# Six row buffers before the scatter, router products in three places, and two groups of stores on other queues, in a gated attention and expert layer

## The chip, the cores and the metric

The kernel runs on one core of a Trainium2 chip. A core has five engines that work side by side and wait for each other through semaphores: TensorE (PE, matrix products), VectorE (DVE), ScalarE (ACT), GpSimd (POOL) and SyncE (SP). Copies between the memory outside (DRAM) and the core (SBUF) are DMAs; each is issued by an instruction on the queue of SP, ACT or POOL, and all of them move through the same 16 DMA engines. Each engine takes its instructions in order. The metric is the device time of one execution in microseconds (us), lower is better.

## The reference: what is computed

The input `x` has 4096 rows of 512. An attention block with a context of 3202 rows comes first, then a layer of eight experts of which each row uses two.

```
Sim  = hc@w1 + hq@w2 + (hc*w3)@hq.T + b          # hc = layernorm(x), hq = context
hq_hat = softmax(Sim) @ hq
hc_bar = softmax(max(Sim)) @ hc                  # one row
x1   = x + tanh(g) * (concat[hc, hq_hat, hc*hq_hat, hc*hc_bar] @ W_qv + b_qv)
logits = layernorm(x1) @ w_router + b_router     # 8 experts, the best 2 of each row
buf[expert, slot] = row                          # a fixed number of slots per expert
out  = x1 + tanh(g2) * (weighted sum of the two experts' gelu MLPs)
```

The capacity of an expert is 1.25 * 4096 / 8 = 640 rows here, in five tiles of 128; a row beyond it is dropped. All arithmetic is in float32.

## The kernel before

The work stands in three parts. Part one (lines 124 to 808) is the attention. The 4096 rows are taken in eight groups `g` of 512, and for each group there are these stages:

- `stage_s(g)` (line 425) computes the transposed similarities `E` for 13 blocks of the context, in seven pairs, by a seven-product scheme (`chain`, line 394), and the column maxima `M`. After the last pair, the maxima are transposed on TensorE (`mps`, line 472), reduced on VectorE (`mt`), spread again by a product with a diagonal (`mbps`, from `diag_rows`, line 155) and copied by ScalarE to `mb`.
- `stage_e(g)` (line 498) subtracts `mb` on VectorE and takes the exponential on ScalarE, tile by tile.
- `stage_v(g)` (line 556) multiplies by the context rows (`vv` for group 0, line 568). ScalarE copies the result to `hqT`, and VectorE forms `hqT*qT` and four sums `hs` (lines 654 to 662).
- `stage_d(g - 1)` (line 697) is the product with `W_qv`; its result `xs` goes to DRAM as `r_d`, four DMAs for a group (line 754).

Group 0 has extra work, because the derived operands that later groups read from DRAM are made there. During `stage_v(0)`, `build_values` and `left_sums` (lines 343 and 333) load 13 pairs of context row tiles (`vcv`), form four sums (`vsv`) on VectorE and store them as `vs_d`. `build_weights` (line 345) does the same four times with rows of `W_qv` (`wc`, `wt`, stored as `wt_d`). The buffers of `vcv` and `wc` are two, and so are those of `vsv` and `wt`. The 21 stores are issued from ScalarE's queue, in between its arithmetic.

`router_weights` (line 228) multiplies the four 512-row parts of `W_qv` by the router weights, so that the logits come out beside `x1` later. For each part there are 16 products of 128x128 by eight columns, all into one PSUM bank `we`. In the kernel before, part 0 stands right after the last similarity, part 1 after the four transposes, and parts 2 and 3 after the diagonal product, all ahead of `vv`. The operands are loaded into SBUF tiles that are not yet used for anything else (tags `hqT`, `xr`, `T2`, `hs`).

Part two (lines 826 to 1044) is the second half of `x1` and the routing. It runs over 32 row tiles in nine steps (seven of four tiles and two of two). For each tile, `tile_mm` (line 872) loads `r` and, once for four tiles, `q2T`; TensorE makes eight products (`x1p`, line 885), VectorE finishes `x1` and its statistics, and ScalarE's queue stores `x1` to `out`. For each step, `norms` (line 906) computes the scale on GpSimd (`rstd`) and writes the normalised rows to `xn`, `route` (line 922) finds the two experts on VectorE, and `dispatch` (line 1017) scatters the rows to their slots in `buf_d` by eight indirect DMAs on GpSimd's queue, two for each tile. The loop at line 1035 calls `norms` for step `g`, then `dispatch` for step `g - 2`, then `route` for step `g - 1`. `xn` has three buffers, the default of the pool. Beside its rows each `xn` holds the token's number, copied there by VectorE (line 1002). The weights of the first expert are loaded along the way, one half after `q2T` 3 and one after `q2T` 6.

Part three (lines 1052 to 1267) runs the eight experts; its loads of `buf_d` wait for all scatters.

What stands where in each engine's queue is decided by a scheduler when the program is built; `tc.issue_after` places an instruction no earlier than another.

Of the kernel before, what the change touches and what calls it, by code (L numbers as in the profile page):

```python
# [6 lines left out]
F32 = mybir.dt.float32  # L7
# [7 lines left out]
P = 128  # L15
# [5 lines left out]
def gated_layer(ctx, tc, x, x_t, ctxt, ctxt_t, g_xattn, g_ffn, w_sim, w_sim1, b_sim, W_qv, W_qv_t, b_qv, b_qv_c, w_router, b_router, w1, b1, w2, b2, out):  # L21
# [14 lines left out]
    TG = 4 * P  # L36

    BW = D // 2 + E // 2
    B1 = D // 2 + E
    NG = N // TG  # L40
# [29 lines left out]
    r_d = [dram.tile([P, 2, BW], F32, name=f"r_d{t}", tag=f"r_d{t}") for t in range(NT)]  # L70

    R = D + 4
# [19 lines left out]
    we = const.tile([P, 4, DC, E], F32, name="we")  # L92
# [31 lines left out]
    with ExitStack() as s1:  # L124
        ee = s1.enter_context(tc.tile_pool(name="ee", bufs=1))
        kv = s1.enter_context(tc.tile_pool(name="kv", bufs=1))
        st = s1.enter_context(tc.tile_pool(name="st", bufs=5))
        sb = s1.enter_context(tc.tile_pool(name="sb1", bufs=1))
# [12 lines left out]
        wt_d = dram.tile([P, 8, DC, BW], F32, name="wt_d", tag="wt_d")  # L141
# [6 lines left out]
        def bank(name):  # L148
            return ps_m.tile([P, 2, 256], F32, name=name, tag="m")
# [10 lines left out]
        live = {}  # L160
# [66 lines left out]

        def router_weights():

            pa_ = sb.tile([P, DC, TG], F32, name="wq0", tag="hqT")  # L230
            pb_ = sb.tile([P, 4, 2, BW], F32, name="wq1", tag="xr").rearrange("p a b c -> p (a b c)")[:, : DC * D]
            parts = [[(pa_, 0, D)], [(pb_.rearrange("p (c f) -> p c f", c=DC), 0, D)], [], []]
            for c in range(DC):
                t2 = ee.tile([P, 2, 256], F32, name=f"wq2_{c}", tag=f"T2{c}").rearrange("p a b -> p (a b)")
                parts[2].append((t2.rearrange("p (c f) -> p c f", c=DC), c * P, P))
            for i, k in enumerate((2, 4)):
                parts[3].append((sb.tile([P, DC, 256], F32, name=f"wq3_{i}", tag=f"hs{k}"), i * 256, 256))
            ps = bank("we").rearrange("p a b -> p (a b)")[:, : 4 * DC * E].rearrange("p (k c e) -> p k c e", k=4, c=DC)
            for k, pieces in enumerate(parts):
                for a, f0, n in pieces:  # L240
                    with tc.issue_after(queue[-1].ins):
                        nc.sync.dma_start(a, W_qv_t[:, :, k * D + f0 : k * D + f0 + n])

            def step(ks):
                for k in ks:
                    for a, f0, n in parts[k]:
                        for f in range(n // P):
                            for d in range(DC):
                                nc.tensor.matmul(
                                    ps[:, k, (f0 // P) + f, :], a[:, d, f * P : (f + 1) * P], wrc[:, d, :],  # L250
                                    start=k == 0 and f == 0 and d == 0, stop=d == DC - 1, skip_group_check=True,
                                )

            return step, lambda: nc.vector.tensor_copy(we, ps)

        def stage_n(g):

# [75 lines left out]
        def left_sums(name, w, vc, dst):  # L333

            vs = sb.tile([P, 4, 256], F32, name=f"vs{name}", tag="vs", bufs=2)
            A11, A21, A12, A22 = (vc[:w, h, c : c + 256] for h in range(2) for c in (0, 256))
            tt(vs[:w, 0, :], A21, A22, ALU.add)
            tt(vs[:w, 1, :], vs[:w, 0, :], A11, ALU.subtract)
            tt(vs[:w, 2, :], A11, A21, ALU.subtract)
            tt(vs[:w, 3, :], A12, vs[:w, 1, :], ALU.subtract)  # L340
            nc.scalar.dma_start(dst, vs[:w])

        def build_values(j):

# [2 lines left out]
        def build_weights(c):  # L347


            vc = sb.tile([P, 2, 2, BW], F32, name=f"wc{c}", tag="vc", bufs=2)  # L350
            for h in range(2):
                with tc.issue_after(queue[-1].ins):
                    nc.sync.dma_start(
                        vc[:, h, :, :256],
                        W_qv[(h + 1) * D + c * P : (h + 1) * D + (c + 1) * P, :].rearrange("p (j d) -> p j d", j=2),
                    )
            nc.vector.tensor_copy(vc[:, :, :, 256:], we[:, 1:3, c, :].rearrange("p h (j e) -> p h j e", j=2))
            nc.scalar.dma_start(wt_d[:, 0:4, c, :], vc.rearrange("p h j d -> p (h j) d"))
            B11, B12, B21, B22 = (vc[:, h, j, :] for h in range(2) for j in range(2))
            wt = sb.tile([P, 4, BW], F32, name=f"wt{c}", tag="vs", bufs=2)  # L360
            tt(wt[:, 0, :], B12, B11, ALU.subtract)
            tt(wt[:, 1, :], B22, wt[:, 0, :], ALU.subtract)
            tt(wt[:, 2, :], B22, B12, ALU.subtract)
            tt(wt[:, 3, :], B21, wt[:, 1, :], ALU.subtract)
            nc.scalar.dma_start(wt_d[:, 4:, c, :], wt)

        def load_keys(g, j):
            kt = st.tile([P, 7, 2, WJ[j]], F32, name=f"kt{g}_{j}", tag="st")
# [56 lines left out]
        def stage_s(g):  # L425
# [39 lines left out]
                    for h in (1, 0):  # L465
                        tt(m, m, e[:w, :, h], ALU.max)  # L466
            if g == 0:
                rw, rw_end = router_weights()
                rw([0])
            ps = ps_tr.tile([P, 4, P], F32, name=f"mps{g}", tag="tr")  # L470
            for i in range(4):
                tr = nc.tensor.transpose(ps[:, i, :], M[:, i // 2, 0, (i % 2) * P : (i % 2 + 1) * P], ident)
            if g == 0:
                with tc.issue_after(tr.ins):
                    rw([1])
            mt = sm.tile([P, 4], F32, name=f"mt{g}", tag="mt")
            nc.vector.tensor_reduce(mt, ps, AX.X, ALU.max)
            ps = ps_tr.tile([P, 4, P], F32, name=f"mbps{g}", tag="tr").rearrange("p a b -> p (a b)")
            dr = diag_rows(ps, f"m{g}", mt)
            if g == 0:  # L480
                with tc.issue_after(dr.ins):
                    rw([2, 3])

            m = sm.tile([P, 4], F32, name=f"m{g}", tag="mm")
            stt(m, qw[:, 4 * g : 4 * g + 4], bsim, mt, ALU.add, ALU.add)
# [7 lines left out]
            nc.scalar.copy(mb.rearrange("p a b -> p (a b)"), ps)  # L493
            live[g]["mt"], live[g]["mb"] = mt, mb
            if g == 0:
                live[g]["we"] = rw_end

        def stage_e(g, first):

# [56 lines left out]
        def stage_v(g, early, between):  # L556
# [6 lines left out]
            def product(ps, what, right, start=True, stop=True):  # L563
                for i in range(2):
                    vt = load_values(g, what, i)
                    for j in range(i * JH, min((i + 1) * JH, NJ)):
                        for b in range(2):
                            nc.tensor.matmul(  # L568
                                ps[b], vt[: WJ[j], j - i * JH, b * P : (b + 1) * P], right(j),
                                start=start and j == 0 and (b == 0 or g == 0), stop=stop and j == NJ - 1,  # L570
                                skip_group_check=True,
                            )

            if g == 0:
                with tc.issue_after(v["last"].ins):
                    v["we"]()
                for i in range(2):
                    ps = [bank(f"vv{i}_{b}") for b in range(2)]
                    for h in range(2):
                        product(  # L580
                            ps, (h, i * 256), lambda j: E[j // 2][: WJ[j], :, h, j % 2, :], start=h == 0, stop=h == 1
                        )
# [114 lines left out]
        def stage_d(g):  # L697
# [53 lines left out]
            prod(pb, "3", start=False)  # L751
            out_sum(pb, u2, 0, 1)
            for i in range(4):
                nc.sync.dma_start(r_d[4 * g + i], xs[:, i, :, :])

# [69 lines left out]
    G = 4  # L825
    with ExitStack() as s2:
# [79 lines left out]
        def norms(k, x1s, mv, lg):  # L906
            n = len(x1s)
            rstd = sm.tile([P, G], F32, name=f"rstd{k}", tag="rstd")[:, :n]
            nc.gpsimd.tensor_scalar(rstd, mv[:, :n, 1], EPS, None, ALU.add)
# [413 lines left out]
```

## Time and profile before

| | |
|---|---|
| median of 3 runs | 2747.27 us (2743.96 to 2749.41) |
| the profiled execution | 2750.92 us |
| its span, first to last instruction | 2749.1 us |
| TensorE busy | 2656.2 us (97%) |
| VectorE busy | 1689.9 us (61%) |
| ScalarE busy | 420.0 us (15%) |
| GpSimd busy | 219.8 us (8%) |
| mean rate of DMA over the span | 159 GB/s |

The profile page and the answers of its trace are about one execution. Times are in microseconds from the start of the span. A row of the timeline has the start, the duration, the engine, the line of the kernel, the operation, what it writes and what it reads, how many such instructions in a row, and in brackets the idle time before it with what ended it. SPq, ACTq and POOL rows with DMA are DMAs as they are issued. A float32 product counts as two matmul rows. PEclk is the share of TensorE's full clock that was granted. A row of the list of waits names the engine and line that waited, what it waited for, the sum, how many times, and the longest.

### The profile page before, as it was taken

How to read it: one execution, taken by the hardware profiler on the slowest of the kernel's cores; microseconds unless marked ns; L12 is line 12 of the kernel's file. 1: busy time of each engine (PE TensorE's matmuls, PEld its weight loads, DVE VectorE, ACT ScalarE, POOL GpSimd, SP SyncE). 2: the span in 40 equal slices, each digit the busy share in tenths (PEclk: the TensorE clock that was granted, in tenths of full speed). 3: DMA queues.
4: the chain of work that ended last, by engine and by line, in shares of the span. 5: the costliest groups of instructions: out<-in, count | busy, mean ns of one | idle time of the engine just before them, and what ended most of it. 6: DMA issues, size and time to landing. Idle time of an engine off the chain costs nothing. (4 is left out here: it accounts for less than half of the span.)

```text
span 2749.1 us, 29996 instructions
## 1 busy us (share of the span) xinstructions
PE 2656.2 (97%) x11384; PEld 2139.7 (78%) x11384; DVE 1689.9 (61%) x3410; ACT 420.0 (15%) x673; POOL 219.8 (8%) x268
## 2 busy tenths in 40 slices
PE   8999999999999999999999985699999999999998
PEld 7847888888888888888888774477777777777776
DVE  6755755946847559468374556555656475756654
ACT  1200200201202002012020011111111212111111
POOL 0000000000001000000000035201010010101010
PEclk9799999999999999999999998899999999999999
DMA  6876766646747657467445684223233231423210
GB/s 250 247 265 216 173 221 156 227 157 175 233 163 173 219 152 231 158 174 231 150 144 180 243 310 156 91 77 100 92 103 118 86 123 62 146 85 108 78 61 20
DMA packets 191908, 436.64 MB, mean 159 GB/s; under 512 B 18599, under 2 KB 95648, under 8 KB 189716
## 3 DMA queue, kind: packets, MB, share of 16 engines
q1 hardware_dynamic: 158114, 358.54, 41.3%
q0 software_dynamic: 13648, 36.55, 4.2%
q10 hardware_dynamic: 20001, 39.63, 3.9%
q8 instruction: 90, 1.47, 0.2%
q14 instruction: 55, 0.44, 0.0%
HBM read 356.22 MB, written 85.60 MB: 161 GB/s over the span
## 5 line engine op out<-in xcount | busy, mean ns | idle before, releaser
L448 PE MATMUL pas<-Qp,kt 128*128 128x256 f32 (+1 forms) x728 | 174.1, 380 | 0.0
L1085 PE MATMUL pah<-bT,w 128*128 128x320 f32 x512 | 160.1, 435 | 0.8 <-DVE bT L1126 0.8
L568 PE MATMUL pbv<-E,vt 128*128 128x256 f32 (+1 forms) x728 | 159.5, 379 | 0.0
L568 PEld LDWEIGHTS pbv<-E,vt 128*128 128x128 f32 (+1 forms) x728 | 138.2, 190 | 18.9
L448 PEld LDWEIGHTS pas<-Qp,kt 128*128 128x128 f32 (+1 forms) x728 | 135.2, 187 | 21.3 <-ACT p1s L405 0.2
L885 PE MATMUL x1p<-W,q2T 128*128 128x264 f32 x512 | 126.6, 411 | 18.9 <-DVE mv L903 12.4
L508 DVE TENSOR_TENSOR E<-E,mb 128x1024 f32<-128x1024 f32 (+1 forms) x112 | 125.0, 1140 | 17.3 <-ACT mb L493 17.3
L509 ACT ACTIVATE E<-E 128x1024 f32<-128x1024 f32 (+1 forms) x112 | 111.4, 996 | 156.4 <-DVE E L508 154.0
L885 PEld LDWEIGHTS x1p<-W,q2T 128*128 128x128 f32 x512 | 103.3, 204 | 39.9 <-issue 20.8
L1085 PEld LDWEIGHTS pah<-bT,w 128*128 128x128 f32 x512 | 97.5, 191 | 39.9 <-DVE bT L1126 1.2
L1085 PE MATMUL pao<-w,h 128*128 128x256 f32 x512 | 121.0, 379 | 0.0
L1237 PE MATMUL op<-w,h 128*128 128x512 f32 x256 | 113.6, 592 | 0.0
L466 DVE TENSOR_TENSOR M<-M,E 128x1024 f32<-128x1024 f32 (+1 forms) x96 | 109.0, 1135 | 6.4
L1260 POOL DMA_INDIRECT out<-acc,ti x40 | 42.8, 1070 | 855.9 <-DVE acc L1259 855.9
L1085 PEld LDWEIGHTS pao<-w,h 128*128 128x128 f32 x512 | 96.7, 190 | 16.7 <-issue 4.3
L405 ACT COPY p1s<-pas 128x512 f32<-128x512 f32 (+1 forms) x56 | 31.1, 555 | 488.4 <-issue 256.7
L421 DVE TENSOR_TENSOR E<-p4s,u3s 128x512 f32<-128x512 f32 (+1 forms) x56 | 36.5, 652 | 107.4 <-PE p4s L448 107.4
L448 PE MATMUL pbs<-Qp,kt 128*128 128x256 f32 (+1 forms) x364 | 88.0, 384 | 4.0 <-DVE E L416 4.0
L520 DVE TENSOR_TENSOR SM<-SM,E 128x1024 f32<-128x1024 f32 (+1 forms) x80 | 88.8, 1110 | 0.0
L1237 PEld LDWEIGHTS op<-w,h 128*128 128x128 f32 x256 | 47.2, 190 | 52.0 <-issue 46.4
L448 PE MATMUL p6s<-q,kt 128*128 128x256 f32 (+1 forms) x364 | 86.6, 379 | 0.0
L448 PE MATMUL pbs<-q,kt 128*128 128x256 f32 (+1 forms) x364 | 86.6, 379 | 0.0
(406 smaller groups left out, 5240.5 us busy)
## 6 DMA issues: line engine op xcount, KB each, us to landing
kt<-kt_d SPq DMA_DIRECT2D x84, 896.0 KB
w<-in_w SPq DMA_DIRECT2D x32, 2048.0 KB
wp<-wt_d SPq DMA_DIRECT2D x56, 520.0 KB
vt<-vs_d SPq DMA_DIRECT2D x28, 896.0 KB
vt<-vs_d SPq DMA_DIRECT2D x28, 640.0 KB
kt_d<-ktb ACTq DMA_DIRECT2D x12, 896.0 KB
buf_d<-zero SPq DMA_DIRECT2D x80, 129.0 KB
xb<-buf_d SPq DMA_DIRECT2D x40, 258.0 KB
```

The lines of the kernel that those rows point to most:

```text
L405: nc.scalar.copy(p1, cut(pa))
L421: tt(done(1, 0), cut(p4), u3, ALU.add)
L448: nc.tensor.matmul(ps[:w, jl, :], kts[j][:, KSLOT[p], k, :], B[p][:, k, :], start=start and jl == 0 and k == 0, stop=stop and k == 1, skip ...
L466: tt(m, m, e[:w, :, h], ALU.max)
L508: live[g]["last"] = tt(e, e, m, ALU.subtract)
L509: live[g]["exp"] = nc.scalar.activation(e, e, AF.Exp)
L520: tt(s, E_t[0][:, lr] if jj == 1 else s, e, ALU.add)
L568: nc.tensor.matmul(ps[b], vt[: WJ[j], j - i * JH, b * P : (b + 1) * P], right(j), start=start and j == 0 and (b == 0 or g == 0), stop=stop ...
L885: nc.tensor.matmul(ps[:, j, :B1], qTs[g][:, c, i * P : (i + 1) * P], W1[:, c, j, :], start=(c == 0), stop=(c == DC - 1))
L1085: nc.tensor.matmul(ps, a, b, start=start and i == 0, stop=stop and i == len(A) - 1, skip_group_check=True)
L1237: nc.tensor.matmul(ps, hT[:, k, 2 * MH :], W2[:, k, :], start=(k == 0), stop=(k == KH - 1))
L1260: sc = nc.gpsimd.indirect_dma_start(out=out[:, :], out_offset=rows_of(ti, s), in_=acc[:, :], in_offset=None, bounds_check=N - 1, oob_is_er ...
```

## The change

There are four edits.

- `xn` gets six buffers.
- The router products are made in three places. Part 1 stands right after the last similarity, part 2 after the diagonal product, both into a bank `we12`; parts 0 and 3 follow the last `vv` product of group 0, into a bank `we03`, ahead of the row sums `rsps` and of `stage_s(1)`. The loads go in the order 1, 2, 0, 3, into other tags than before. In place of one copy of the bank to `we` there are three copies on VectorE, two of them at the end of `stage_v(0)`.
- The 13 stores of `vs_d` and the eight of `wt_d` are issued from GpSimd's queue.
- The four stores of `r_d` of the last group are issued from ScalarE's queue.

```diff
@@ router_weights @@
-            pa_ = sb.tile([P, DC, TG], F32, name="wq0", tag="hqT")
...
+            parts = [[], [], [], []]
+            a = sb.tile([P, DC, TG], F32, name="wq1", tag="hqT")
+            parts[1].append((a, 0, D))
+            a = sb.tile([P, 4, 2, BW], F32, name="wq2", tag="xr").rearrange("p a b c -> p (a b c)")[:, : DC * D]
+            parts[2].append((a.rearrange("p (c f) -> p c f", c=DC), 0, D))
+            for i, k in enumerate((2, 4)):
+                parts[0].append((sb.tile([P, DC, 256], F32, name=f"wq0_{i}", tag=f"hs{k}"), i * 256, 256))
             for c in range(DC):
...
+                parts[3].append((t2.rearrange("p (c f) -> p c f", c=DC), c * P, P))
+            for k in (1, 2, 0, 3):
...
-            def step(ks):
+            def step(ps, ks, first=True):
...
+        def we_bank(name):
+            return bank(name).rearrange("p a b -> p (a b)")[:, : 4 * DC * E].rearrange("p (k c e) -> p k c e", k=4, c=DC)
@@ left_sums @@
-            nc.scalar.dma_start(dst, vs[:w])
+            nc.gpsimd.dma_start(dst, vs[:w])
@@ build_weights @@
-            nc.scalar.dma_start(wt_d[:, 0:4, c, :], vc.rearrange("p h j d -> p (h j) d"))
+            nc.gpsimd.dma_start(wt_d[:, 0:4, c, :], vc.rearrange("p h j d -> p (h j) d"))
...
-            nc.scalar.dma_start(wt_d[:, 4:, c, :], wt)
+            nc.gpsimd.dma_start(wt_d[:, 4:, c, :], wt)
@@ stage_s @@
-                rw, rw_end = router_weights()
-                rw([0])
+                rw, rps = router_weights(), we_bank("we12")
+                rw(rps, [1])
...
-            if g == 0:
-                with tc.issue_after(tr.ins):
-                    rw([1])
...
                 with tc.issue_after(dr.ins):
-                    rw([2, 3])
+                    rw(rps, [2], False)
@@ stage_v @@
                 with tc.issue_after(v["last"].ins):
-                    v["we"]()
+                    nc.vector.tensor_copy(we[:, 1:3], rps[:, 1:3])
...
+                with tc.issue_after(vv.ins):
+                    rps = we_bank("we03")
+                    rw(rps, [0])
+                    rw(rps, [3], False)
+                    nc.vector.tensor_copy(we[:, 0], rps[:, 0])
+                    nc.vector.tensor_copy(we[:, 3], rps[:, 3])
                 between()
@@ stage_d @@
-                nc.sync.dma_start(r_d[4 * g + i], xs[:, i, :, :])
+                (nc.scalar if g == NG - 1 else nc.sync).dma_start(r_d[4 * g + i], xs[:, i, :, :])
@@ norms @@
-            xg[k] = sb.tile([P, G, R], F32, name=f"xn{k}", tag="xn")
+            xg[k] = sb.tile([P, G, R], F32, name=f"xn{k}", tag="xn", bufs=6)
```

More of the change, by code (lines that the diff above doesn't have):

```diff
@@ L228, in router_weights @@
         def router_weights():
-            pa_ = sb.tile([P, DC, TG], F32, name="wq0", tag="hqT")
-            pb_ = sb.tile([P, 4, 2, BW], F32, name="wq1", tag="xr").rearrange("p a b c -> p (a b c)")[:, : DC * D]
-            parts = [[(pa_, 0, D)], [(pb_.rearrange("p (c f) -> p c f", c=DC), 0, D)], [], []]
-            for c in range(DC):
[L234 to L240, printed above, removed]
+            parts = [[], [], [], []]
[5 more added lines that the diff above has]
+                parts[0].append((sb.tile([P, DC, 256], F32, name=f"wq0_{i}", tag=f"hs{k}"), i * 256, 256))
+            for c in range(DC):
+                t2 = ee.tile([P, 2, 256], F32, name=f"wq3_{c}", tag=f"T2{c}").rearrange("p a b -> p (a b)")
+                parts[3].append((t2.rearrange("p (c f) -> p c f", c=DC), c * P, P))
+            for k in (1, 2, 0, 3):
+                for a, f0, n in parts[k]:
                     with tc.issue_after(queue[-1].ins):
                         nc.sync.dma_start(a, W_qv_t[:, :, k * D + f0 : k * D + f0 + n])
-            def step(ks):
+            def step(ps, ks, first=True):
                 for k in ks:
@@ L250, in step @@
                                     ps[:, k, (f0 // P) + f, :], a[:, d, f * P : (f + 1) * P], wrc[:, d, :],
-                                    start=k == 0 and f == 0 and d == 0, stop=d == DC - 1, skip_group_check=True,
-                                )
-            return step, lambda: nc.vector.tensor_copy(we, ps)
+                                    start=first and k == ks[0] and f0 == 0 and f == 0 and d == 0, stop=d == DC - 1,
+                                    skip_group_check=True,
+                                )
+            return step
+        def we_bank(name):
+            return bank(name).rearrange("p a b -> p (a b)")[:, : 4 * DC * E].rearrange("p (k c e) -> p k c e", k=4, c=DC)
         def stage_n(g):
@@ L495, in stage_s @@
             if g == 0:
-                live[g]["we"] = rw_end
+                live[g]["we"] = rw, rps
         def stage_e(g, first):
@@ L567, in product @@
                         for b in range(2):
-                            nc.tensor.matmul(
+                            mm = nc.tensor.matmul(
                                 ps[b], vt[: WJ[j], j - i * JH, b * P : (b + 1) * P], right(j),
@@ L572, in product @@
                             )
+                return mm
             if g == 0:
+                rw, rps = v["we"]
                 with tc.issue_after(v["last"].ins):
-                    v["we"]()
+                    nc.vector.tensor_copy(we[:, 1:3], rps[:, 1:3])
                 for i in range(2):
@@ L579, in stage_v @@
                     for h in range(2):
-                        product(
+                        vv = product(
                             ps, (h, i * 256), lambda j: E[j // 2][: WJ[j], :, h, j % 2, :], start=h == 0, stop=h == 1
```

## The prediction, as put on record

> **What bounds the kernel now.** I read the page's 40 slices first. TensorE is full except in three places: the slice from about 1580 to 1760 us, its neighbours, and a dip of its clock near 100 to 140 us.
>
> ```profile
> PE   8999999999999999999999985699999999999998
> PEclk9799999999999999999999998899999999999999
> DMA  6876766646747657467445684223233231423210
> ```
>
> So the page says "TensorE-bound", and only these places have time to give. In each I look for the wait that ends last. For 1540 to 1740, the list of waits of that stretch has two entries that hold TensorE back and that this change touches:
>
> ```profile
> DVE xn L1002 <- DMA buf_d<-xn,sidx: 35.1, 5, 11.0
> PE x1p L885 <- DMA q2T<-qT_d: 5.3, 1, 5.3
> ```
>
> The first is VectorE, held at the copy of the token number until the scatter three steps back has landed. The timeline shows one step on GpSimd and VectorE:
>
> ```profile
> 1592.76 0.22 POOL L909 TENSOR_SCALAR rstd<-mv 128x4 f32<-128x4 f32 x1 [12.89 <-DVE tmp L984]
> 1598.53 1.15 POOL L1020 DMA_INDIRECT buf_d<-xn,sidx  x1 [4.44 <-DVE mv L903]
> 1607.69 0.97 POOL L1020 DMA_INDIRECT buf_d<-xn,sidx  x1 [0.30 <-issue]
> 1614.76 0.17 DVE L1002 COPY xn<-tok 128x4 f32<-128x4 f32 x1 [10.46 <-DMA buf_d<-xn,sidx]
> 1616.66 0.23 POOL L909 TENSOR_SCALAR rstd<-mv 128x4 f32<-128x4 f32 x1 [8.00 <-DVE tmp L984]
> ```
>
> GpSimd ends its eight scatters at 1608.66, idles 8.00 us, and starts the next `rstd` after VectorE is freed. The second wait starts on SP, whose queue has `r_d` stores ahead of the first `q2T` load:
>
> ```profile
> 1535.56 3.83 SPq L754 DMA_DIRECT2D r_d<-xr  x3
> 1539.48 0.38 SPq L876 DMA_DIRECT2D q2T<-qT_d  x1
> ```
>
> Around 100 us, TensorE's own timeline:
>
> ```profile
> 101.29 4.62 PE L249 MATMUL we<-wrc,wq 128*128 128x8 f32 x32
> 105.76 1.09 PE L472 MATMUL mps<-ident,M 128*128 128x128 f32 x4
> 106.65 6.83 PE L249 MATMUL we<-wrc,wq 128*128 128x8 f32 x32
> 113.33 2.05 PE L155 MATMUL mbps<-dgm,ones 128*128 128x512 f32 x2
> 115.18 13.66 PE L249 MATMUL we<-wrc,wq 128*128 128x8 f32 x64
> 128.69 15.11 PE L568 MATMUL vv<-E,vt_(0_0)_0_918 128*128 128x512 f32 x28
> ...
> 236.30 3.29 PE L448 MATMUL pbs<-Qp,kt 128*128 128x256 f32 x8 [3.96 <-DVE E L416]
> ```
>
> The router products fill 101 to 128.7 without a gap, part of it in front of the diagonal product on which all exponentials wait. At the far end of stage V, TensorE idles 3.96 us.
>
> **What the skill says.** "TensorE: Matmul & The Clock Gate", section What's actually happening: TensorE runs at half clock after an idle window of some 3.4 us, and at full clock after about as much sustained work. The trace agrees in size: the granted clock falls to 0.50 in the slice from 104 us, 2.6 us after the eight-column products begin, and is back at 1.00 from 135, 5.9 us after `vv` began. That products so narrow count as idle is shown by this trace, not by the page. "DMA: Bandwidth & Descriptors", section Issuing engines are not separate DMA queues: DMAs of SP, ACT and POOL share 16 engines, so another queue saves issue time only. Hence I give the moved stores no faster transfer. "SBUF — State Buffer", section SBUF: two separate sides: a VectorE instruction in a two-port mode keeps GpSimd from writing descriptors. The large VectorE rows of stage V are two-input `TENSOR_TENSOR`, which that page's section Who interferes with whom gives no such mode. No run here shows stores of this shape from GpSimd.
>
> **Six buffers.** The `rstd` of steps 2 to 7 start at 1592.76, 1616.66, 1641.13, 1661.16, 1681.51 and 1697.29. The first four periods are 23.90, 24.47, 20.03, 20.35 us; VectorE's waits within them are 10.46, 11.01, 6.57, 6.92. What is left is 13.4 each, so without the wait VectorE would do a step in 13.4. But GpSimd is next: from `rstd` to the first scatter 5.77 (VectorE's slot arithmetic lies between), then eight scatters, 1598.53 to 1608.66, 10.13; after that the next `rstd`. That is 15.9, and the fifth period, 15.78, already runs at it. In the built program's list of waits, the token copies of steps 3 to 5 wait for no scatter any more, those of 6 to 8 for scatters three steps older. So four periods become 15.85: 88.75 - 63.4 = 25.3 us, not the 35.1 of the list. From step 7 on GpSimd issues without a pause, unchanged to 1733.36.
>
> DMA may take some back. The windows view gives 229 GB/s over 1540 to 1740, 45.8 MB. A four-tile step moves q2T 1.05, r 1.06, x1 1.05 and scatters 2.11 MB by the sizes in the issue list, 5.27 MB; two steps with the second weight half (4.2 MB) make 14.7 MB in 31.7 us, 465 GB/s, where the best ten-us slice had 404 and good ones 380. At 380 that is 7 us late. The weights aren't urgent, but stand in SP's queue ahead of later `r` loads; three buffers of `r` are 3 x 3.6 us of cover. I take a loss of 3, between 0 and 13. Gain 22.3.
>
> **Last rows from ScalarE.** TensorE ends stage D's last product at 1539.63 (16 rows from 1536.13 at the pace of the rows before, 3.50) and begins `x1p` at 1545.05. In the built order the `q2T` load follows `br` (1524.01) and waits for old work only, so it lands during stage D. That frees 5.4 us, and the clock does not dip: the first 63 rows took 17.18, at the pace of the next 140 (31.31) 14.1, so 3.1 more. ScalarE's queue has nothing to do until 1552.60; four issues of some 0.4 us cost nothing there. Gain 8.4; 5 if the clock dips all the same.
>
> **Router products.** Part 1 still costs 4.47 at 101.29 and the transposes 0.89. Then the diagonal product waits for VectorE only (reduction 106.89, product 107.62 + 0.69): 108.35, 1.85 long. Part 2 follows, 6.68, to 116.9. In the trace the first exponential ends 5.1 after the diagonal product's start, here 113.4, so `vv` starts at 116.9 instead of 128.69: 11.8 earlier. `vv` lasts 92.2 as before, to 209.1. Parts 0 and 3 are 64 rows: 18 at 0.140 until the clock falls after 2.5 us, 46 at 0.211, 12.2 in all, to 221.3; with `rsps` 222.3. Stage S's second group began at 221.72 before. Its first pair, 12.1 at full clock, now loses 2.9 at half clock (half of 5.9) but not the 3.96 idle: next pair at 237.3. Before it came at 239.39, with 0.43 of half clock left. Gain 2.5. The two small copies that VectorE makes of the late bank, 0.2 each, are a new wait: behind them stand the reciprocal of `rsps`, which comes after those products on TensorE anyway, and the four sums, so they hold nothing longer. The loads of the four parts only change order within SP's 75 to 89 us and cost nothing. If the clock holds throughout, 64 rows take 9.0 and nothing is lost after: gain 8.6. If VectorE is as late as now, -3.
>
> **Stores from POOL.** They are off ScalarE, whose copies of `hqT` stood behind them until 227.00 though `vv` ended at 221. On GpSimd nothing else is queued behind them until its row at 274.50, so 21 issues of 0.6 to 1.2 us (its rows here) are hidden. The sums now begin 11.8 earlier and end near 215 if the round trip stays; VectorE then needs 6.9 for `hqT*qT`, copies and sums, and stage S first needs it at 229. So 7 us of slack cover slower landings. No gain of its own counted.
>
> **Sum.** 22.3 + 8.4 + 2.5 = 33.2 from the profiled 2750.9 (span 2749.1 and 1.8 around it): 2717.7. The median lies 3.6 below the profiled execution: 2714.1.
>
> **Rivals.** A, as above, 2714; alone 2708 to 2720; chance 0.58. B, DMA becomes the bound of routing: the 7 us are not hidden and two gaps bring half clock, 2.9 each, 13 lost instead of 3: 2724. For it: 465 GB/s wanted; against: the first weight half passed at 283 to 404 GB/s without a TensorE gap, though beside no scatter. 0.25. C, the clock holds through the last router products (+6.1) and DMA costs nothing (+3): 2705. Against: the drop at 104. 0.13. D, slower: the POOL stores land late. Of GpSimd's DMAs the 4 KB `mr_d` takes 14.0 us to land, though the 512 KB `mrb` 6.3. Seventeen tiles pass two buffers; now 93.2 us, 11 per use of a buffer. From 121.5 on, with a cycle of 17 they end at 266, 44 later than stage S can bear: 2758. It outweighs everything from a cycle of 15.7. Against: `mr_d` is in 4-byte pieces, the stores are in kilobytes. 0.04. That nothing changes is excluded by the built order.
>
> Measurement tells about 0.2% (5.5 us) from no change. B may end there once in 25: faster 0.95, same 0.01, slower 0.04. The range 2704 to 2727 takes in A, B and C.
>
> **What would show it.** Periods of `rstd` of 15.9 with no scatter wait on VectorE; `x1p` beginning at D's end; `vv` 11.8 earlier, the late products in 12 us at half clock. I am wrong if `r` loads hold VectorE at line 889, or if `vsv` waits for stores longer than now.

## The result, and the profile after

The changed kernel takes 2713.7 us in the median of four runs (2711.54 to 2717.1), against 2747.27 before: a ratio of 0.988, 95% interval 0.9863 to 0.9897. Its profiled execution takes 2714.11, its span 2712.3. The span is 36.8 shorter than that of before, the median 33.6; the profiled execution of before lay 3.6 above its median, that of the changed kernel 0.4 above its own.

Line numbers of the changed kernel are up to 10 higher (those of the experiments up to 18 more), so `x1p` at L885 is now L895, `rstd` L919, the token copy L1012, the scatter L1030.

The page's slices, in the same order as before:

```profile
PE   8999999999999999999999994899999999999999
PEclk9898999999999999999999997899999999999999
DMA  7984765646746657467445794222323132322210
```

TensorE's three low slices, 8 5 6 before, are 4 8 now: there is less idle time, and it stands in one piece. Just ahead of it DMA reads 7 9 4 where it read 6 8 4: the same bytes of the routing go through in less time.

The list of waits from 1530 to 1700 (engine, line, what it waited for, sum, times, longest). The token copy's entry, 35.1 before, and the `q2T` entry are gone:

```profile
DVE lg L922 <- POOL rstd L920: 24.6, 9, 4.9
POOL buf_d L1030 <- DVE gate L957: 20.0, 4, 5.1
...
DVE x L899 <- DMA r<-r_d: 7.1, 2, 6.0
```

GpSimd's timeline for the steps that it bounds:

```profile
1577.26 0.22 POOL L919 TENSOR_SCALAR rstd<-mv 128x4 f32<-128x4 f32 x1 [12.89 <-DVE tmp L994]
1583.56 1.15 POOL L1030 DMA_INDIRECT buf_d<-xn,sidx  x1 [4.96 <-DVE left L966]
...
1593.69 0.26 POOL L919 TENSOR_SCALAR rstd<-mv 128x4 f32<-128x4 f32 x1
...
1613.34 0.23 POOL L919 TENSOR_SCALAR rstd<-mv 128x4 f32<-128x4 f32 x1 [3.35 <-DVE tmp L994]
```

The first step starts the next `rstd` the moment its eighth scatter is issued: GpSimd is the bound. The second does not: it idles 3.35, because VectorE had waited 6.0 for a row `r`.

In both steps the first scatter comes 6.3 after `rstd`, where the prediction took 5.77 from the kernel before. VectorE's order shows where that comes from. The last row that VectorE writes into `xn` for a scatter is `xn<-gv,wsum`; in all these steps, before and after, the first scatter starts 0.76 to 0.85 after that row ends. (The profile names other rows as what ended the idle time; the constant lag points to this one.) In the kernel before it stands ahead of the statistics `st` of the next tile:

```profile
1597.51 0.17 DVE L998 TENSOR_TENSOR xn<-gv,wsum 128x8 f32<-128x8 f32 x1
1597.58 0.69 DVE L902 BATCH_NORM_STATS2 st<-x 128x6 f32<-128x512 f32 x1
```

In the changed kernel it stands behind them, 0.6 later, counted from `rstd`:

```profile
1598.44 0.69 DVE L912 BATCH_NORM_STATS2 st<-x 128x6 f32<-128x512 f32 x1
1599.04 0.15 DVE L1008 TENSOR_TENSOR xn<-gv,wsum 128x8 f32<-128x8 f32 x1
```

SP's queue at the seam of the two parts:

```profile
1517.45 0.37 SPq L886 DMA_DIRECT2D q2T<-qT_d  x1
```

TensorE there:

```profile
1529.04 3.67 PE L720 MATMUL pbd<-wp,hs 128*128 128x260 f32 x16
1532.55 42.88 PE L895 MATMUL x1p<-W,q2T 128*128 128x264 f32 x192
```

The load is issued 15 us before `x1p` needs it, and 192 rows follow without idle time at full clock. And TensorE around stage V of group 0:

```profile
98.66 3.63 PE L250 MATMUL we<-wrc,wq 128*128 128x8 f32 x32
102.15 0.63 PE L477 MATMUL mps<-ident,M 128*128 128x128 f32 x4
104.29 2.08 PE L155 MATMUL mbps<-dgm,ones 128*128 128x512 f32 x2 [1.51 <-DVE dgm L154]
106.15 6.83 PE L250 MATMUL we<-wrc,wq 128*128 128x8 f32 x32
112.84 14.44 PE L570 MATMUL vv<-E,vt_(0_0)_0_886 128*128 128x512 f32 x28
...
204.38 12.20 PE L250 MATMUL we<-wrc,wq 128*128 128x8 f32 x64
```

**Where the 36.8 lie.** Five marks divide the span. (1) The first router product comes at 98.66 in place of 101.29, 2.6 earlier. Nothing ahead of it was changed but the order and the places of four loads, and kernels with this part untouched have it anywhere from 98.2 to 101.3: chance. (2) From there to the transposes `mps` of group 1 the changed kernel needs 202.29 where the one before needed 206.76 (they begin at 300.95 and 308.05): 4.5. Each of the six groups after that takes 183.91 in both. (3) From the start of stage D's last products to the first `rstd`: 28.22 before, 19.75 now, 8.5. (4) From the third `rstd` to the eighth: 104.53 before, 85.45 now, 19.1. (5) From the eighth `rstd` to the end of GpSimd's scatters: 36.06 before, 34.51 now, 1.5. The experts give 0.7.

### The profile page after: what moved, and what is told of

Its sections match the earlier page's. It is cut to its first block, busy times and chain, and to the rows that moved or that the text cites. A ratio compares the mean times of both kernels' runs of the same rounds, so it can differ in the third digit from the quotient of the medians.

```text
span 2712.3 us, 29984 instructions
## 1 busy us (share of the span) xinstructions
PE 2642.9 (97%) x11384; PEld 2130.5 (79%) x11384; DVE 1689.3 (62%) x3412; ACT 419.8 (15%) x673; POOL 233.2 (9%) x289
## 5 line engine op out<-in xcount | busy, mean ns | idle before, releaser
L570 PEld LDWEIGHTS pbv<-E,vt 128*128 128x128 f32 (+1 forms) x728 | 138.2, 190 | 18.9
L510 DVE TENSOR_TENSOR E<-E,mb 128x1024 f32<-128x1024 f32 (+1 forms) x112 | 125.2, 1142 | 12.4 <-ACT mb L495 12.4
L895 PE MATMUL x1p<-W,q2T 128*128 128x264 f32 x512 | 118.0, 391 | 3.3 <-DVE wsum L1007 1.6
L895 PEld LDWEIGHTS x1p<-W,q2T 128*128 128x128 f32 x512 | 97.7, 192 | 21.2 <-PE x1p L895 3.6
```

What stands on the lines that cost most here:

```text
L510: live[g]["last"] = tt(e, e, m, ALU.subtract)
L570: mm = nc.tensor.matmul(ps[b], vt[: WJ[j], j - i * JH, b * P : (b + 1) * P], right(j), start=start and j == 0 and (b == 0 or g == 0), stop ...
L895: nc.tensor.matmul(ps[:, j, :B1], qTs[g][:, c, i * P : (i + 1) * P], W1[:, c, j, :], start=(c == 0), stop=(c == DC - 1))
```

## The experiments

Each kernel was timed beside the kernel before, and its ratio is to that, with a 95% interval. The kernel before had medians from 2747.27 to 2749.89 in these comparisons, so the difference of two medians from different comparisons is uncertain by some 3 us (an estimate from these medians). Where that is too coarse, the comparisons below use the trace's own stretches.

**Six buffers alone.**

```diff
-            xg[k] = sb.tile([P, G, R], F32, name=f"xn{k}", tag="xn")
+            xg[k] = sb.tile([P, G, R], F32, name=f"xn{k}", tag="xn", bufs=6)
```

> The kernel before with one edit: six xn buffers. Prediction's theory: the steps of the routing become bound by GpSimd at 15.85 us, less a loss to DMA contention; the trace of the changed kernel gives 19.1 for these periods and 1.5 for the last ones, so 2727 us (20.6 faster). Rival 1: all of the listed wait of 35.1 us is gained, 2712. Rival 2: the buffers alone bring less, because the second weight half collides with the row loads harder when the first q2T load is late: 2735 or more.

2728.06 us, ratio 0.9927 (0.9914 to 0.9941), 20 faster: as the theory had it, not the 35.1 of the list. The profiled execution lies 4.0 above this median; in it the five periods are 15.7 shorter than before and the tail behind them 0.7. From the third `rstd` to the eighth it takes 88.84, 3.4 more than the changed kernel. VectorE's list of waits over the routing says why:

```profile
DVE x L889 <- DMA r<-r_d: 9.4, 1, 9.4
```

One row load is later than in the changed kernel (6.0), and one period becomes 23.02 in place of 19.65.

**Last rows from ScalarE alone.**

```diff
-                nc.sync.dma_start(r_d[4 * g + i], xs[:, i, :, :])
+                (nc.scalar if g == NG - 1 else nc.sync).dma_start(r_d[4 * g + i], xs[:, i, :, :])
```

> The kernel before with one edit: the last group's four r_d stores from ScalarE's queue. Theory: x1p begins at the end of stage D without a gap and at full clock, 8.4 us faster, 2739. Rival 1: the clock dips all the same, 5 faster, 2742. Rival 2: the routing waits for its scatters anyway (xn copies), and gives the early start back: 2745 to 2747.

2742.5 us, ratio 0.9978 (0.9969 to 0.9988). The stretch from stage D's last products to the first `rstd` is 19.80, 8.4 shorter, and `x1p` begins without idle time; the routing behind it (105.27 for the five periods, 104.53 before) gives nothing back. The median shows only 5.4. The first rival had named that time, 2742, but not its cause: the clock does not dip, it is 1.00 from 1536 to 1560. In the profiled execution 2.9 are lost far from the edit, in the second group's first similarities:

```profile
228.06 1.99 PE L448 MATMUL pas<-Qp,kt 128*128 128x256 f32 x8 [1.54 <-ACT p1s L405]
```

That wait differs between executions of kernels with the same code there (none before, 1.61 in the run with six buffers), so it isn't the edit's. How much of the median's shortfall it explains is not shown.

**Router products alone**, with the 21 stores on ScalarE's queue as before: the changed kernel with the other three edits undone.

```diff
-            nc.gpsimd.dma_start(dst, vs[:w])
+            nc.scalar.dma_start(dst, vs[:w])
...
-                (nc.scalar if g == NG - 1 else nc.sync).dma_start(r_d[4 * g + i], xs[:, i, :, :])
+                nc.sync.dma_start(r_d[4 * g + i], xs[:, i, :, :])
...
-            xg[k] = sb.tile([P, G, R], F32, name=f"xn{k}", tag="xn", bufs=6)
+            xg[k] = sb.tile([P, G, R], F32, name=f"xn{k}", tag="xn")
```

> The kernel before with one edit: the router products in three places; the stores stay on ScalarE's queue. Prediction's theory: vv begins 11.8 earlier, 12.2 come back after it, and the gain is 2.5, 2745. Rival 1: ScalarE's copies of hqT still stand behind the stores, VectorE and TensorE are as late as before at the second group's first pair, and nothing is gained or 3 are lost: 2747 to 2750. Rival 2: all of what the changed kernel has gained by 232 us (7.1) comes from here: 2740.

2745.36 us, ratio 0.999 (0.9983 to 0.9996): 2.5 faster. From the first router product to the transposes of group 1 it takes 202.50, against 206.76 before and 202.29 in the changed kernel. ScalarE's queue shows that the copies of `hqT` still stand behind the stores:

```profile
224.03 0.37 ACTq L370 DMA_DIRECT2D wt_d<-wt  x1
224.44 1.07 ACT L595 COPY hqT<-vv 128x512 f32<-128x512 f32 x2 [44.22 <-DMA kt<-kt_d]
```

They come 17 us after the end of `vv` (207.6), and yet TensorE has no gap:

```profile
232.37 1.89 PE L453 MATMUL p4s<-q,kt 128*128 128x256 f32 x8
234.09 1.89 PE L453 MATMUL pbs<-Qp,kt 128*128 128x256 f32 x8
```

So the first rival falls. The margin is small: VectorE's sum that this last product waits for ends at 233.48, 0.6 before.

**Stores from GpSimd's queue alone.**

```diff
-            nc.scalar.dma_start(dst, vs[:w])
+            nc.gpsimd.dma_start(dst, vs[:w])
...
-            nc.scalar.dma_start(wt_d[:, 4:, c, :], wt)
+            nc.gpsimd.dma_start(wt_d[:, 4:, c, :], wt)
```

> The kernel before with one edit: the 21 stores from GpSimd's queue. Prediction's theory: no gain of its own, 2747. Rival 1: the 3.96 us idle of TensorE ahead of the second group's similarities are a wait for the hqT copies behind the stores on ScalarE, and go: 2743. Rival 2: stores land later from GpSimd's queue and VectorE waits longer: over 2750.

2748.83 us, ratio 1.0002 (0.9993 to 1.001): nothing. `hqT` is now copied as soon as `vv` ends (213.84), and the idle time stays:

```profile
230.77 3.78 PE L448 MATMUL pbs<-Qp,kt 128*128 128x256 f32 x8 [4.86 <-DVE E L416]
```

The gap was not the copies behind the stores. VectorE's last weight sum, held up by the load of `wc`, ends at 222.2 here; then come `hqT*qT`, the four sums and three sums of the similarities. TensorE needs the last of these, which ends at 230.7. What closes the gap is the block of router products that now stands in front of the similarities.

**The last rows on SP again**, in the changed kernel.

```diff
-                (nc.scalar if g == NG - 1 else nc.sync).dma_start(r_d[4 * g + i], xs[:, i, :, :])
+                nc.sync.dma_start(r_d[4 * g + i], xs[:, i, :, :])
```

> The changed kernel with one edit undone: the last group's four r_d stores from SyncE's queue again. Theory: the end of stage D to the first rstd takes 25 again in place of 16.3, and the routing steps suffer as in the run with six buffers alone (88.8 from the third to the eighth rstd, not 85.5): 2713.7 + 8.7 + 3.4 = 2726. Rival: the edit is worth only what the run with that edit alone showed in its median (5.4), 2719.

2724.9 us, ratio 0.9916 (0.9903 to 0.993): 11.2 slower than the changed kernel, so the rival falls. From stage D's last products to the first `rstd` it takes 28.91, 9.2 more; the five periods take 86.20, 0.8 more, not the 3.4 of the run with six buffers alone. The lateness of that one row load differs between executions: its period was 19.65, 20.41 and 23.02 in the three kernels.

**The second weight half later.**

```diff
-                if g in (3, 6):
+                if g == 3:
                     with tc.issue_after(ld.ins):
-                        load_half(0, g // 6)
+                        load_half(0, 0)
...
-            nc.sync.dma_start(r, r_d[t])
+            ld = nc.sync.dma_start(r, r_d[t])
+            if t == NT - 1:
+                with tc.issue_after(ld.ins):
+                    load_half(0, 1)
```

> The changed kernel with the second half of the first expert's weights issued behind the last row load, in place of behind the seventh q2T load. Theory: the one long rstd period (19.65) is r loads behind that half; it becomes 16.4 like its neighbours, no r load holds VectorE at line 899, and 3.3 are gained: 2710.4. Rival 1: DMA is full in this stretch whatever the order; another period gets long and nothing is gained: 2713 to 2715. Rival 2: the weights now come too late for the first expert: over 2716.

2712.42 us, ratio 0.9868 (0.9853 to 0.9884). No row load holds VectorE, and the long period is gone:

```profile
1593.63 0.26 POOL L922 TENSOR_SCALAR rstd<-mv 128x4 f32<-128x4 f32 x1
1609.96 0.27 POOL L922 TENSOR_SCALAR rstd<-mv 128x4 f32<-128x4 f32 x1
1626.29 0.27 POOL L922 TENSOR_SCALAR rstd<-mv 128x4 f32<-128x4 f32 x1
```

Five periods take 82.23, 3.2 less. DMA by ten-us slices (the last columns are the granted clock, the DMA share and GB/s), 1600 to 1630, in the changed kernel:

```profile
1600.00:1610.00 10.00, 10.00 (x49) 8.60 (x48) 5.21 (x23) 0.00 (x0) 7.86 (x8) 1.00 1.03 412
1610.00:1620.00 10.00, 8.10 (x36) 6.35 (x35) 7.16 (x47) 3.05 (x5) 1.69 (x3) 1.00 1.04 407
1620.00:1630.00 10.00, 9.16 (x44) 7.84 (x43) 6.78 (x28) 0.00 (x0) 7.76 (x10) 1.00 1.04 408
```

The same slices with the weights late:

```profile
1600.00:1610.00 10.00, 10.00 (x49) 8.60 (x48) 7.06 (x29) 0.00 (x0) 7.86 (x9) 1.00 0.94 312
1610.00:1620.00 10.00, 10.00 (x49) 8.60 (x48) 8.29 (x55) 3.05 (x5) 4.31 (x5) 1.00 0.92 311
1620.00:1630.00 10.00, 10.00 (x47) 8.54 (x46) 5.82 (x32) 1.92 (x3) 6.19 (x7) 1.00 0.85 312
```

So the contention is real, and it is the weights. Of the 3.2 only 1.7 are left in the span and 1.3 in the median. The experts' part, from the last scatter to the end, is 1.5 longer here. But it varies as much without this edit: it takes 1014.6 to 1016.7 in the traces with the weights in their old place, and 1014.9 in the last run below, which moves them too. A cost of the later weights is not shown.

**Four buffers, and five.**

```diff
-            xg[k] = sb.tile([P, G, R], F32, name=f"xn{k}", tag="xn", bufs=6)
+            xg[k] = sb.tile([P, G, R], F32, name=f"xn{k}", tag="xn", bufs=4)
```

> The changed kernel with four xn buffers in place of six. Theory: with three, a token copy waits for scatters that GpSimd has just issued; with four, for those of a period before (some 16 us, against some 10 of landing), so no wait is left, and the time is that of six: 2713 to 2715. Rival: landing takes longer when DMA is full, and VectorE waits at the token copy again in the full periods: 2718 or more.

2729.37 us, ratio 0.993 (0.9916 to 0.9943): my theory is wrong. VectorE waits again, four times and 14.4 in all; the two longest are:

```profile
1600.94 0.17 DVE L1012 COPY xn<-tok 128x4 f32<-128x4 f32 x1 [5.43 <-DMA buf_d<-xn,sidx]
1622.63 0.17 DVE L1012 COPY xn<-tok 128x4 f32<-128x4 f32 x1 [5.29 <-DMA buf_d<-xn,sidx]
```

The built order explains it. Once a buffer is free in time, the scheduler puts the token copy of a step right behind the `rstd` product of the step before: the copy moves one step ahead, and takes back one buffer. With four, the copy at 1595.5 wants scatters whose last was issued at 1592.62 and which land at 1600.94. The rival named the right time, but slower landing is hardly the cause: these land 7.3 after the last issue ends, against 6.1 at the first wait of the kernel before. If it is the order, five are enough:

```diff
-            xg[k] = sb.tile([P, G, R], F32, name=f"xn{k}", tag="xn", bufs=6)
+            xg[k] = sb.tile([P, G, R], F32, name=f"xn{k}", tag="xn", bufs=5)
```

> The changed kernel with five xn buffers in place of six. Theory after the run with four: VectorE copies the token number of a step one step ahead of its rows, so with four buffers it waits for scatters that GpSimd has issued in the step just past (landed 1600.9, 7.3 after the last issue); with five they have landed some 11 us before the copy. So no scatter wait on VectorE and the time of six: 2712 to 2715. Rival: it is DMA that is slow in this stretch, and each buffer less costs something: 2718 or more.

2714.69 us, ratio 0.9886 (0.9871 to 0.9901), no scatter wait on VectorE, five periods in 85.11: five do what six do.

**Slot arithmetic ahead of the `rstd` product.** If GpSimd bounds a step because it idles 4.9 between `rstd` and the first scatter, then taking that idle time away must shorten the step.

```diff
-                norms(g, [tile_mm(t, mv, lgs[g]) for t in STEPS[g]], mv, lgs[g])
-            if half_routed is not None:
-                dispatch(g - 2, half_routed())
+                x1s = [tile_mm(t, mv, lgs[g]) for t in STEPS[g]]
+            sidx, end = half_routed() if half_routed is not None else (None, None)
+            if g < len(STEPS):
+                pw = norms(g, x1s, mv, lgs[g], end)
...
+            if sidx is not None:
+                with tc.issue_after(pw.ins):
+                    dispatch(g - 2, sidx)
...
-            nc.vector.tensor_tensor(l_, l_, rstd.unsqueeze(2).to_broadcast([P, n, E]), ALU.mult)
+            with tc.issue_after(after.ins) if after is not None else ExitStack():
+                nc.vector.tensor_tensor(l_, l_, rstd.unsqueeze(2).to_broadcast([P, n, E]), ALU.mult)
```

Here `end` (`after` within `norms`) is the last operation of the slot arithmetic, and `pw` the last of `rstd` on GpSimd.

> The changed kernel with the slot arithmetic of a step on VectorE ahead of the multiplication that waits for rstd, and the scatters on GpSimd held behind that rstd. Theory: GpSimd bounds a step at 16.4 because it idles 4.9 between rstd and the first scatter; this idle goes, GpSimd needs 11.8, and the step falls to TensorE's 14.2 unless DMA (some 400 GB/s at best) is the next bound: 2700 with DMA free, 2708 if DMA takes half. Rival: GpSimd's step was not the bound, DMA was: 2713 to 2715 and longer waits for r loads.

2712.13 us, ratio 0.987 (0.9855 to 0.9885): little, for the edit did only half of what it was to do. `nb`, which waits for `rstd` too, still stood ahead of the slot arithmetic, and the idle time fell from 4.9 only to 4.1 to 4.3. The periods that no row load held became 15.5 to 15.7. The step with the late row load is still 20.16. The next kernel puts all three operations behind it, by moving two lines up into the block that is already held back, and the second weight half late as above:

```diff
             with tc.issue_after(after.ins) if after is not None else ExitStack():
+                nc.vector.scalar_tensor_tensor(nb, mv[:, :n, 0], -1.0, rstd, ALU.mult, ALU.mult)
                 nc.vector.tensor_tensor(l_, l_, rstd.unsqueeze(2).to_broadcast([P, n, E]), ALU.mult)
+                nc.vector.tensor_tensor(l_, l_, br.unsqueeze(1).to_broadcast([P, n, E]), ALU.add)
...
```

> The changed kernel with the slot arithmetic ahead of all three VectorE operations that wait for rstd, nb among them, and the second weight half behind the last row load. Theory: GpSimd needs 1.3 for rstd, some 2 of waiting and 10.1 for the scatters, 13.3 a step; TensorE's 14.2 becomes the bound, five periods take 71 to 74 in place of 85.5, and the time is 2700 to 2704. Rival: at 14.2 a step DMA has to move 371 GB/s and more; it becomes the bound, r loads hold VectorE, and no more is gained than by the weights and the first reordering together (2.7 and 3.2): 2708 to 2710.

2707.51 us, ratio 0.9852 (0.9835 to 0.9868), 6.2 faster than the changed kernel. The periods are 14.73, 14.65, 14.68, 14.69 and 14.63; TensorE is busy for all of each ten-us slice from 1550 to 1650:

```profile
1594.17 0.26 POOL L922 TENSOR_SCALAR rstd<-mv 128x4 f32<-128x4 f32 x1
...
1598.63 1.08 POOL L1034 DMA_INDIRECT buf_d<-xn,sidx  x1 [3.06 <-ACT xn L932]
...
1608.82 0.23 POOL L922 TENSOR_SCALAR rstd<-mv 128x4 f32<-128x4 f32 x1 [0.16 <-DVE tmp L999]
```

GpSimd now waits 0.16 for VectorE's statistics, which follow TensorE. TensorE goes from step to step without idle time:

```profile
1592.49 14.49 PE L898 MATMUL x1p<-W,q2T 128*128 128x264 f32 x64
1607.18 14.49 PE L898 MATMUL x1p<-W,q2T 128*128 128x264 f32 x64
```

A step of TensorE takes 14.69, and that is the period: the bound has changed hands. (The expected 14.2 left out the 0.36 of the two `pos` products between the steps.) GpSimd, which still idles 3.06 before its first scatter, is only 0.16 behind. The rival (DMA) falls: from 1600 to 1620 DMA is about as full as in the changed kernel (share 1.04 and 1.01, 378 and 375 GB/s), and no row load holds VectorE. The five periods gain 12.1 on the changed kernel's, as expected. The tail after the eighth `rstd` is 2.4 longer, which the expected 2700 to 2704 left out, and the experts' part 1.5, which is within what it varies by. So 8.2 are left from the first `x1p` to the end.

**Late router products spread.** Three products at a time stand behind each of the first eleven products of the second group's similarities.

```diff
-                with tc.issue_after(vv.ins):
-                    rps = we_bank("we03")
-                    rw(rps, [0])
-                    rw(rps, [3], False)
...
+                            with tc.issue_after(mm.ins):
+                                for _ in zip(range(3), late):
+                                    pass
```

> The changed kernel with the router products of parts 0 and 3 spread, three at a time, between the first eleven products of the second group's similarities, in place of one block behind vv. Theory: it is the unbroken run of eight-column products that lets the clock fall; spread, the clock stays, 64 rows cost 9.0 in place of 12.2, the 2.9 of half clock after them and 0.9 at rsps go, and VectorE's lateness stays covered: 6 to 7 faster than the changed kernel, 2707. Rival 1: the narrow products pull the clock down between wide ones too: 2714 or more. Rival 2: VectorE is now late for the third pbs, and TensorE idles there as before the change: 2711 to 2713.

2713.16 us, ratio 0.9871 (0.9853 to 0.9889): no difference that the medians show. The trace splits it in two. The clock holds at 1.00 from 200 to 225, where it was 0.50 to 0.60 from 205 to 220 in the changed kernel. From the first router product to the transposes of group 1 it takes 199.82, 2.5 less. But VectorE is late, as the second rival had it:

```profile
215.94 0.51 PE L253 MATMUL we<-wrc,wq 128*128 128x8 f32 x4
...
225.90 3.61 PE L466 MATMUL pbs<-Qp,kt 128*128 128x256 f32 x8 [3.73 <-DVE E L425]
```

**The last two kernels' edits together.**

> The slot arithmetic ahead, the second weight half late and the router products of parts 0 and 3 between similarities, all three on the changed kernel. Theory: the places are apart and the gains add: 2707.5 less the 2.5 that the trace showed for the spread router products between the two rows of transposes (196.3 in place of 198.8): 2705. Rival: what is gained there is lost again or is chance of the clock: 2707 to 2709.

2701.82 us, ratio 0.9839 (0.9822 to 0.9857), the fastest kernel of this study: 12 faster than the changed kernel, 5.7 faster than without the spreading. The last difference is not clear of noise: the intervals of the two ratios overlap, and each set against the kernel before in its own comparison it is 3.6. Here VectorE was in time but for 0.30:

```profile
225.19 1.99 PE L466 MATMUL pbs<-Qp,kt 128*128 128x256 f32 x8 [0.30 <-DVE E L425]
```

and from the first router product to the transposes of group 1 it takes 195.84, 6.4 less than in the changed kernel, as the theory of the spread products had it. But the gains do not simply add. The five periods take 77.08, 3.7 more than without the spreading. In the longest of them, 17.95, VectorE stands still once, and the profile does not say for what ("remote"):

```profile
1587.72 0.75 DVE L917 SCALAR_TENSOR_TENSOR x<-x1p,gx,r 128x512 f32<-128x512 f32 x1 [4.53 <-remote]
```

In stage V of group 0, VectorE ends the last weight sum at 217.2 in the run that only spreads the products and at 216.5 here, at the pace of loads and stores, while TensorE comes to the third `pbs` at 222.2 and 224.9: a few us decide whether it waits. That may be why the runs of these two kernels spread over 8 and 14 us; it isn't shown.

## Why the prediction was right, point by point

The time (2714.1 said, 2713.7 measured) is nearer than the steps are: the buffers gave 1.7 less than said and the router products 2.0 more. The mechanism of each step was right; that the sum is 0.4 off is luck.

- **Six buffers: 22.3 said, 20.6 measured (19.1 in the five periods, 1.5 in the tail).** Right in kind: not the 35.1 of the list, since GpSimd comes next, and the reordered kernels, which shorten the step by freeing GpSimd, show that it was the bound. One term of the sum was mis-sized, "four periods become 15.85": those without a late row are 16.27 to 16.56, since the first scatter comes 6.3 to 6.5 after `rstd`, not 5.77. The prediction took this stretch as fixed, but with more buffers the scheduler put a row that the scatter needs behind the 0.69 of `st` (above). Over five periods that is about 3. The loss to DMA, "3, between 0 and 13", was 3.3 in the changed kernel (19.65 against 16.3), 3.2 by the run that moves the weights, and 6.7 in the run with six buffers alone. The tail's 1.5 were not foreseen. Alone, the edit gave 20 in the median, but only 16.4 of it lie in these stretches of its profiled execution.
- "I am wrong if `r` loads hold VectorE at line 889": they did, 6.0 at one place. It was the price already in the sum, so the condition was put too strictly.
- **Last rows from ScalarE: 8.4 said, 8.5 measured,** 8.4 in the edit alone and 9.2 when undone: the idle 5.4 went, and the 192 rows behind it took 42.72 in place of 45.72.
- **Router products: 2.5 said, 4.5 measured** from the first router product to the transposes of group 1, 4.3 with this edit alone. `vv` began 13.2 earlier, counted from the first router product, not 11.8, in the main because that first part stayed at full clock and took 3.49 in place of 4.47; and `vv` itself took 91.5, not 92.2. These two make up the 2.0. "12.2 in all" for the late block was 12.20, but by two errors that cancel. The 0.140 for a row at full clock is the mean of 32 rows in which the clock fell after 2.4 us; at full clock throughout, 32 rows took 3.49, so 0.109 each. And the clock fell 1.6 us into the late block, not 2.5. When it falls differs by execution. In the run with the slot arithmetic ahead it fell only after 4.8 us, and the same block was shorter:

```profile
206.24 9.27 PE L250 MATMUL we<-wrc,wq 128*128 128x8 f32 x64
```

So the gain is no fixed number: the stretch took 205.3 to 209.6 in the four kernels with the old order, 200.2 to 203.5 in the eight with the new block. That the late block covers VectorE's lateness, and the gap of 3.96 goes for that reason, is shown by the two single edits and by the spread products, with which the gap came back.
- **Stores from GpSimd: nothing said, nothing measured,** alone (1.0002) or beside the router products (202.50 without, 202.29 with). They took 0.70 to 0.82 each to issue and 5.8 to 7.6 to land, in the median of each kind. "7 us of slack" was not needed. `vsv` did wait longer for stores than before (18.9 in place of 13.1 over 110 to 230 us), which I had called a sign of being wrong. No time was lost by it: with `wt`, VectorE's waits for stores rose from 17.7 to 19.9, and its waits for loads fell from 24.1 to 17.2.
- **Rival B** (DMA bounds the routing) had the right place and the wrong size; **C** said that a clock that holds is worth 6.1 more. Its 9.0 for 64 rows at full clock was too much (0.113 a row makes 7.2), and to hold the clock throughout took another order of the products, which gained 6.4; **D** needed stores that land late, and they did not.

The four edits one by one sum to 27 in medians, not 33.6. Most of the shortfall stands at one edit: the last rows from ScalarE gave 5.4 alone, and cost 11.2 when undone. The late row and the second group's similarities, which differ by execution, may account for much of that, and the four intervals allow the rest (1.8 to 3.7 either way for each); it was not separated.

## What to carry to other kernels

A wait that the profile lists is worth what the next-slowest engine leaves of it: write down that engine's own work per step before claiming the sum. A buffer count is only as good as the order that the scheduler makes of it, so look at where the freed instruction lands in the built order. And when an engine's step is short work around one wait, put all that does not need the awaited value ahead of all that does: with one operation that needed it left in front, the idle time fell only from 4.9 to between 4.1 and 4.3.

## What the runs showed of the hardware

- TensorE's clock fell to half while 64 matmul rows of eight columns ran in one block, 1.6 to 4.8 us after the block began (12.20 in the changed kernel, granted clock 0.50 from 206). It stayed at 1.00 when six such rows at a time stood between pairs of 256-column rows: the twelve pairs of wide rows and 64 narrow ones took 12.4, and less the wide rows' 5.2 (24 at 0.2155) that is 0.113 a narrow row. "TensorE: Matmul & The Clock Gate" in the Trainium skill (section What's actually happening) ties half clock to an idle window of some 3.4 us; here the trace lists TensorE as busy for all of 205 to 215, and the clock fell all the same.
- From 1600 to 1630 of the changed kernel, with 4.2 MB of weights queued ahead of row loads, the 16 DMA engines delivered 407 to 412 GB/s (share 1.03 to 1.04), and one row load held VectorE for 6.0 us. With the weights late, none did, at 311 to 312 GB/s and also at 375 to 378 in the run with the slot arithmetic ahead (share 1.01 to 1.04).
